# Head, tail and order of work of a four-stage sequence kernel: dummies and x, field 14's sums, and a table of shifts for the planner

## The chip, the cores and the metric

The kernel runs on one core of one Trainium2 chip. The metric is device microseconds (us) of one execution, the median of several. In the text PE is TensorE's matmuls and PEld its weight loads, DVE is VectorE, ACT is ScalarE, POOL is GpSimd and SP is the queue of SyncE, which here issues most DMA transfers.

## The reference

The input x holds 16 batches of 256 rows by 256 columns, float32. Four layers follow each other; each batch is independent, so a batch can be in one layer while the next is still in an earlier one.

```python
# layer 0: adapter with an expert per batch, residual, layer norm
hidden = gelu(x @ down_W.T + down_b)                       # 64 wide
hidden = hidden @ expert_W[idx].T + expert_b[idx] + domain_emb[idx]
x = ln(hidden @ up_W.T + up_b + x) * ln_gamma + ln_beta
# layer 1: transformer block, 16 heads of 16, scale and shift from a timestep
xn = ln(x) * (1 + scale) + shift
p = softmax(where(mask, -inf, q @ k.T / 4 + attention_bias))
x = xn + (p @ v) @ Wo + bo
x = x + gelu2((ln(x) * g2 + beta2) @ W1 + b1) @ W2 + b2    # 1024 wide
# layer 2: one of three branches per batch, residual, layer norm
y = ln(x + branch[c](x)) * gamma + beta
# layer 3: y as a 256 x 256 field, one explicit time step
df = -(grad(A0*y, 1) + grad(A1*y, 2)) + 0.5 * (grad2(B0*y, 1) + grad2(B1*y, 2) + 2 mixed terms of B2*y)
out = maximum(y + df * dt, 0)
```

The attention bias is the large operand: 16 x 16 x 256 x 256 float32.

## The kernel before

**Chains and a planner.** The work is written as ten Python generators, called chains: adapt and prepare (layer 0), project, weigh, attend, mask and divide (attention), enter and feed (its feed-forward half), end (layer 2) and step (layer 3). Each writes the instructions of its stage for batch after batch and stops at every `yield`, which names the time when its next piece can start and how many PSUM banks it needs. The class Flow (L99) keeps a clock for each engine and for the DMA engines, advanced by a fixed cost for each piece (`flow.dve(0.66)` and the like). `run` (L163) chooses which chain goes on: among those whose next piece can start by TensorE's planned clock, those in a hurry first, then the one with the lowest position `c[2]`; with none ready, the one that can start first. A position starts at a constant and grows with the TensorE time that the chain has spent (L1388 on, `flow.add(project(), -0.03998, 9.784)`: start, and TensorE us per unit of position). So the planner only fixes the order in which instructions are written. On the chip every engine runs its own instructions in that order, and waits by semaphores.

**PSUM and TensorE.** Seven banks are given out by `misc` and returned by `free`; an eighth holds the attention sums. A float32 product is two instructions of TensorE. Instructions named idle (L229 to L242) are products of zeros, which compute nothing that is used: they read `c_va`, two tiles that DVE clears at the start.

**The head.** The first batch goes through its stages nearly alone: w_down, xt and tokens are loaded; p_h (L565) is the first product, gelu follows on ACT, p_e (L580) needs the expert's weights, whose DMA (L323) needs the token's index, p_u (L596) leads back to 256 columns, and x is added on DVE (L604) after POOL has added up_b to it (`biased`, L550). `prepare` takes the means and variances (L438, L439), POOL makes rs from them (L442, L443), and then come `silus`, `condition` (ps_a, L521, which reads w_ada) and three dummies of 512 columns. `project` starts with the transposes c_t (L485) of c_ln. Loads of the head go out on SP's and ACT's queues in the order of the code: x of batch 0 on SP, behind xt; w_ada on ACT, ahead of rows_a.

**The body.** weigh writes the scores of four heads (c_s, L837 or L850), DVE adds the bias and takes the maximum (L870), ACT takes the exponential (L881); attend transposes (c_pt), copies to c_pts on DVE or ACT and multiplies with the values (c_c, L932). project makes q, k and v; from batch 1 on its halves go through DMA transfers (c_st, L658) before weigh can use them. feed has d_f (L1044), tanh, L1068 on DVE, and d_o (L1076) with the addition to y on DVE (L1085). end has d_g, gelu, d_y and the addition to y (L1218), and the means and variances for the last layer.

**The tail.** step works the fields. For fields 0 to 14 (loop at L1309) the normalization ends on POOL (L477, L478), and POOL makes all products and differences: w and a0 (L1318, L1319), a0's sums (L1322, L1323) and edges (L1274 to L1276), b0, p, q, w's sum and edges, and o (L1338). TensorE multiplies with the stencils (`along` L1286, `across` L1296), DVE adds w and the growth (`grown`, L1300, L1301), ACT clips, and SP's queue writes out. For field 14 the TensorE part is held back until end has done batch 15. Field 15 is written out by hand: its normalized field f lies in PSUM (`normalized_affine` with hurry: four instructions on DVE, L468 and L471), ACT copies it to y, DVE makes b0, a0, a0's sums through ps_w in PSUM, and POOL makes p, q and w at the same time; four dummies (`awake`, L1236) stand between field 14's products and its own.

Of the kernel before, what the change touches and what calls it, by code (L numbers as in the profile page):

```python
# [17 lines left out]
ALU = mybir.AluOpType  # L18
# [78 lines left out]


class Flow:  # L99

# [6 lines left out]
    def __init__(self, banks):  # L107
        self.clock = dict.fromkeys(self.LAG, 0.0) | {"SP": 15.5, "DMA": 22.0}
        self.chains = []
        self.after = self.spent = 0.0  # L110
        self.free_at = [0.0] * banks
        self.table = None
# [49 lines left out]

    def run(self):  # L163
        while self.chains:
            open_ = [c for c in self.chains if c[4] is None or c[4]()]
            assert open_, "no chain can go on"
            now = self.clock["PE"] + 0.02818
            ready = [c for c in open_ if self.start(c) <= now]
            if ready:
                c = min(ready, key=lambda c: (not c[5], c[2]))  # L170
            else:
                c = min(open_, key=lambda c: (self.start(c), not c[5], c[2]))
            self.after, self.spent = max(c[1][0], self.clock["PE"] if not ready else 0.0), 0.0
# [13 lines left out]
def chain_kernel(ctx: ExitStack, tc: tile.TileContext, t: dict, out: bass.AP):  # L187
# [39 lines left out]
    vas = [fixed(f"c_va{i}", [P, NC, H // 2, 4, HD]) for i in range(2)]  # L227
    for va in vas:
        nc.vector.memset(va, 0.0)  # L229
# [11 lines left out]
    idles = []  # L241
    idle(512, 384)  # L242

# [20 lines left out]
    def load_x(b):  # L264
        arrives["x", b] = flow.dma(0.8, freed.get(("x", b - 3), 0.0)) if b > 1 else 0.0
        xs[b] = xp.tile([P, NC, D], F32, name=f"x{b}", tag="x", bufs=3)
        nc.sync.dma_start(out=xs[b], in_=t["x"][b])

# [7 lines left out]
    w_ada = wp.tile([P, NC, 2 * D], F32, name="w_ada", tag="d_w", bufs=1)  # L276
    nc.scalar.dma_start(out=w_ada, in_=chunked(t["W_ada"]))
    smalls = hp.tile([P, NC * S], F32, name="smalls", tag="d_ln", bufs=1)
# [106 lines left out]

    rows_a = load("rows_a", rows(t["rows_a"]), [P, 5 * D])
    ln0_g, ln0_b, bv, bo, up_b = (rows_a[:, i * D : (i + 1) * D] for i in range(5))
    w_qkv = fixed("w_qkv", [P, NC, 3 * D])
# [220 lines left out]
    def prepare():  # L609
        for b in range(B):  # L610
# [10 lines left out]
            if b == 0:  # L621
                silus()
                condition()
                idle(512, 512, 512)
            yield at, 0
# [467 lines left out]
    ones = fixed("ones", [1, P])  # L1093
    nc.vector.memset(ones, 1.0)
    chosen = {}
# [130 lines left out]
    def step():  # L1226
# [81 lines left out]
        both = slice(0, NC)  # L1308
        for b in range(B - 1):  # L1309
            yield lambda: ("branch", b) in done  # L1310
# [29 lines left out]
            yield at_b  # L1340
            last = b == B - 2
            if last:
                yield lambda: ("branch", B - 1) in done
            ps_d = misc(f"e_d{b}", [P, NC, S])
            along(ps_d, h_m, b0, start=True)
            for w_, src in ((h_m, b0), (g_m, a0)):
                across(ps_d, w_, src)
            along(ps_d, g_m, a0, stop=True)
            at = flow.pe(2.93)
            if not last:  # L1350
                yield max(at, at_r), 0, True
                free(f"e_d{b}", grown(b, ps_d, w, o, both, 1.42, max(at, at_r)))
                done.add(("step", b))

        n = B - 1
        y, stat, at_y = stats3.pop(n)
        f, ps_w, ps_l = (misc(name, [P, NC, S]) for name in ("e_f", "e_ps_w", f"e_d{n}"))
        tmp, b0_, a0_, p_, q_, w_ = (wide(f"e_{x}{n}") for x in ("tmp", "b0", "a0", "p", "q", "w"))
# [4 lines left out]
        nc.scalar.copy(y, f)  # L1363
        flow.act(0.6, at_f)
        nc.vector.tensor_tensor(b0_, f, b0_g, ALU.mult)
        along(ps_l, h_m, b0_, start=True)
        across(ps_l, h_m, b0_)
        flow.pe(1.5, flow.dve(0.66, at_f))
        nc.gpsimd.tensor_tensor(p_, y, p_g, ALU.mult)
        nc.gpsimd.tensor_tensor(q_, y, q_g, ALU.mult)  # L1370
        nc.gpsimd.tensor_tensor(w_[:, :, mid], p_[:, :, right], q_[:, :, left], ALU.add)
        edges(nc.gpsimd, "r", n, y, edge_r, w_)
        at_w = flow.pool(4.5, flow.clock["ACT"])
        nc.vector.tensor_tensor(ps_w, f, w_g, ALU.mult)
        nc.vector.tensor_tensor(a0_, f, a0_g, ALU.mult)
        nc.vector.tensor_tensor(a0_[:, :, mid], a0_[:, :, mid], ps_w[:, :, right], ALU.add)
        nc.vector.tensor_tensor(a0_[:, :, mid], a0_[:, :, mid], ps_w[:, :, left], ALU.subtract)
        edges(nc.vector, "z", n, f, edge_z, a0_)
        across(ps_l, g_m, a0_)
        along(ps_l, g_m, a0_, stop=True)  # L1380
        at_l = flow.pe(1.4, flow.dve(3.2))
        grown(b, ps_d, w, o, both, 1.42, max(at, at_r))
# [14 lines left out]
    flow.add(step(), 4.348, 57.82)  # L1397
    flow.run()

# [87 lines left out]
```

## Time and profile before

| what | us |
|---|---|
| median of 3 runs (lowest, highest) | 825.84 (824.91, 828.47) |
| the profiled execution | 826.82 |
| its span, first to last instruction | 825.0 |
| TensorE busy in the span | 777.7 |
| mean granted TensorE clock | 0.981 |
| granted clock at one half, in the span | 12.6 to 26.2, 77.4 to 80.8, from 811.3 on |
| DMA traffic | 186.80 MB, mean 226 GB/s |

The page gives each engine's busy time, the span in 40 slices of 20.6 us with a digit for tenths of busy time, and the chain of work that ended last, followed back from the last instruction. Other views are the timeline, the busy time of each engine by stretches, and the waits with the instruction that ended them. A releaser is inferred, and a wait for several things is put down to the last of them.

### The profile page before, as it was taken

How to read it: one execution, taken by the hardware profiler on the slowest of the kernel's cores; microseconds unless marked ns; L12 is line 12 of the kernel's file. 1: busy time of each engine (PE TensorE's matmuls, PEld its weight loads, DVE VectorE, ACT ScalarE, POOL GpSimd, SP SyncE). 2: the span in 40 equal slices, each digit the busy share in tenths (PEclk: the TensorE clock that was granted, in tenths of full speed). 3: DMA queues.
4: the chain of work that ended last, by engine and by line, in shares of the span. 5: the costliest groups of instructions: out<-in, count | busy, mean ns of one | idle time of the engine just before them, and what ended most of it. 6: DMA issues, size and time to landing. Idle time of an engine off the chain costs nothing. (4 is left out here: it accounts for less than half of the span.)

```text
span 825.0 us, 17511 instructions
## 1 busy us (share of the span) xinstructions
PE 777.7 (94%) x5680; PEld 590.4 (72%) x5680; DVE 564.2 (68%) x1964; ACT 598.4 (73%) x1668; POOL 528.3 (64%) x726
## 2 busy tenths in 40 slices
PE   6987999999899999999999999999999999999995
PEld 3565777676677777777777778777777877778772
DVE  6576878787578695678777667766758666747335
ACT  2486889777678586979787579868778787768330
POOL 2437857865777657686266645929292496786885
PEclk8899999999999999999999999999999999999996
DMA  8979799699789988999976998589999989751110
GB/s 291 353 221 277 220 295 294 199 256 252 215 221 275 245 235 256 251 274 273 271 217 199 252 268 261 162 255 254 247 243 290 257 226 257 188 151 46 38 46 26
DMA packets 79242, 186.80 MB, mean 226 GB/s; under 512 B 8473, under 2 KB 22699, under 8 KB 71083
## 3 DMA queue, kind: packets, MB, share of 16 engines
q1 hardware_dynamic: 46192, 120.52, 42.7%
q0 software_dynamic: 31680, 62.92, 35.4%
q10 hardware_dynamic: 1275, 2.19, 0.7%
q8 instruction: 48, 0.79, 0.4%
q14 instruction: 47, 0.39, 0.1%
HBM read 94.90 MB, written 4.19 MB: 120 GB/s over the span
## 5 line engine op out<-in xcount | busy, mean ns | idle before, releaser
L881 ACT ACTIVATE c_pr<-c_pr,c_mx 128x256 f32<-128x256 f32 x512 | 254.8, 500 | 59.9 <-DVE c_mx L870 56.2
L870 DVE CUSTOM_DVE_ANT_0 c_pr<-c_s,side 128x256 f32<-128x256 f32 x512 | 190.8, 417 | 26.9 <-PE c_s L850 6.9
L485 PE MATMUL c_pt<-ident,c_pr 128*128 128x128 f32 x1024 | 155.5, 278 | 5.5 <-ACT d_ht L1021 1.0
L485 PEld LDWEIGHTS c_pt<-ident,c_pr 128*128 128x128 f32 x1024 | 116.5, 140 | 45.7 <-issue 17.1
L1044 PE MATMUL d_f<-d_ht,w 128*128 128x256 f32 x512 | 123.0, 383 | 2.4 <-ACT c_pts L495 0.8
L1076 PE MATMUL d_o<-w,d_z 128*128 128x256 f32 x512 | 120.6, 381 | 0.0
L493 DVE COPY c_pts<-c_pt 128x512 f32<-128x512 f32 x122 | 83.0, 685 | 52.8 <-PE c_pt L485 51.6
L442 POOL TENSOR_SCALAR rs<-mv 128x2 f32<-128x2 f32 x64 | 14.2, 221 | 162.7 <-DVE mv L439 157.1
L538 POOL DMA_DIRECT2D side<-neg x60 | 80.6, 1376 | 41.9 <-DMA side<-in_side 14.1
L1044 PEld LDWEIGHTS d_f<-d_ht,w 128*128 128x128 f32 x512 | 92.4, 190 | 17.5 <-DVE c_mx L870 2.5
L1076 PEld LDWEIGHTS d_o<-w,d_z 128*128 128x128 f32 x512 | 93.2, 190 | 11.7 <-issue 0.4
L881 ACT ACTIVATION_READ_ACCUMULATOR c_pr<-c_pr,c_mx 128x1 f32 x512 | 96.9, 189 | 0.0
L495 ACT COPY c_pts<-c_pt 128x512 f32<-128x512 f32 x134 | 76.7, 575 | 21.0 <-PE c_pt L485 20.6
L932 PE MATMUL c_c<-c_pts,c_va 128*32 128x256 f32 x1024 | 71.7, 385 | 6.3 <-ACT c_pts L495 3.4
L932 PEld LDWEIGHTS c_c<-c_pts,c_va 128*32 128x32 f32 x1024 | 27.6, 109 | 36.3 <-issue 13.3
L1068 DVE SCALAR_TENSOR_TENSOR d_z<-d_f,d_z 128x512 f32<-128x512 f32 x64 | 43.6, 680 | 12.3 <-ACT d_f L1064 12.0
L443 POOL TENSOR_TENSOR rs<-rs,inv_sqrt 128x2 f32<-128x2 f32 x64 | 46.1, 721 | 5.3
L850 PE MATMUL c_s<-c_st 32*128 32x256 f32 x960 | 46.9, 303 | 1.4 <-DVE x L604 0.5
L850 PEld LDWEIGHTS c_s<-c_st 32*128 32x128 f32 x960 | 33.5, 183 | 20.3 <-issue 11.5
L1064 ACT ACTIVATE d_f<-d_z 128x512 f32<-128x512 f32 x64 | 38.3, 598 | 10.3 <-DVE d_z L1061 8.5
L1061 DVE TENSOR_SCALAR d_z<-d_f,cols 128x256 f32<-128x256 f32 x82 | 35.8, 478 | 12.6 <-PE d_f L1044 12.5
L870 DVE DVE_READ_ACCUMULATOR2_ANT c_mx<- 128x1 f32 x512 | 42.5, 83 | 0.0
(195 smaller groups left out, 1490.9 us busy)
## 6 DMA issues: line engine op xcount, KB each, us to landing
side<-in_side SPq DMA_DIRECT2D x63, 1024.0 KB, 6.1
side<-neg POOLq DMA_DIRECT2D x60, 1024.0 KB, 10.2
c_st<-c_qk SPq DMA_DIRECT2D x60, 192.0 KB, 6.1
d_w<-in_W_branch SPq DMA_DIRECT2D x16, 512.0 KB, 6.0
c_st<-c_qk SPq DMA_DIRECT2D x60, 128.0 KB, 6.1
xt<-in_x_t SPq DMA_DIRECT2D x16, 256.0 KB, 5.2
x<-in_x SPq DMA_DIRECT2D x16, 256.0 KB, 5.4
c_st<-c_qk SPq DMA_DIRECT2D x60, 64.0 KB, 5.8
```

What stands on the lines that cost most here:

```text
L443: nc.gpsimd.tensor_tensor(rs, rs, inv_sqrt, ALU.pow)
L485: nc.tensor.transpose(ps[:, k, c * P : (c + 1) * P], src[:, c, k * P : (k + 1) * P], ident)
L493: nc.vector.tensor_copy(dst, ps)
L495: nc.scalar.copy(dst, ps)
L538: nc.gpsimd.dma_start(out=sides[m].rearrange("p (h c) k -> p h (c k)", h=HB), in_=negs[m // 4].rearrange("p c k -> p (c k)").unsqueeze(1). ...
L850: nc.tensor.matmul(ps[i][:, c, :], stacked[rows32, par, 0, c * P : (c + 1) * P], stacked[rows32, par, part, :], start=part == 1 and m not ...
L870: nc.vector.tensor_tensor_reduce(out=pr[:, c, :], in0=ps[i][:, c, :], in1=sb[:, i * NC + c, :], scale=-1.0, scalar=3.0e38, op0=ALU.add, op ...
L881: nc.scalar.activation(pr[:, c, :], pr[:, c, :], AF.Exp, bias=mx[:, c : c + 1], scale=-1.0, accum_out=sums[:, c, h : h + 1],)
L932: nc.tensor.matmul(ps_c[32 * i : 32 * i + 32, :], va[:, k, 4 * half + i, 2 * par : 2 * par + 2, :].rearrange("p e d -> p (e d)"), turned[i ...
L1044: nc.tensor.matmul(ps_f[:, i, :], w1[:, k, f * P : (f + 1) * P], h_t[:, k, :], start=k == 0, stop=k == NC - 1,)
L1068: nc.vector.scalar_tensor_tensor(z, ps_f, 1.0, z, ALU.add, ALU.mult)
L1076: nc.tensor.matmul(ps_o, us[f // 2][:, f % 2, c * P : (c + 1) * P], w2[:, f, :], start=f == 0, stop=f == NF - 1,)
```

## The change

It has four parts.

1. Head. The clearing of the two `c_va` tiles is swapped, so that the one that the dummies read comes first. The dummies ahead of p_h become three of 512 columns (512 and 384 before), those after `condition` four (three before). x of batch 0 is loaded by GpSimd's queue, w_ada goes out behind rows_a, and the tile of ones is set on GpSimd.
2. Field 14 is taken out of the loop and worked as field 15 is: f and ps_w in PSUM, its sums on DVE, p, q and w on GpSimd, o on DVE. Helpers `on_pool`, `on_dve` and `whole` hold what both fields, or the loop, share. What was in the loop for fields 0 to 13 stays.
3. `run` gets a table of 76 entries (plan time, chain, amount). When TensorE's planned clock reaches an entry's time, the amount is added to the position of that chain. Half of the amounts are smaller than 0.81 in size; the largest are those shown. Summed by chain: project +16.7, prepare +5.5, weigh +3.4, attend +0.2, feed -0.3, adapt -1.1, step -2.0, end -3.0, enter -5.3.
4. The planner's clocks start at 4.2 (0 before), SP's at 17.0 (15.5), that of the DMA engines at 23.0 (22.0).

```diff
+SHIFTS = [
+    (4.9, "weigh", -1.29),
+    (5.8, "prepare", 1.69),
+    (19.1, "end", -1.22),
+    (36.8, "weigh", 0.91),
+    (47.8, "end", -0.82),
+    (50.3, "project", 7.46),
+    (50.8, "enter", -0.03),
+    (63.7, "attend", 5.57),
+    (92.3, "step", 0.09),
+    (93.2, "attend", -2.73),
...
+    (160.3, "project", 6.37),
...
+    (841, "step", -2.69),
+]
...
-        self.clock = dict.fromkeys(self.LAG, 0.0) | {"SP": 15.5, "DMA": 22.0}
+        self.clock = dict.fromkeys(self.LAG, 4.2) | {"SP": 17.0, "DMA": 23.0}
...
-    def run(self):
+    def run(self, shifts=()):
+
+        shifts = list(shifts)
         while self.chains:
+            while shifts and shifts[0][0] <= self.clock["PE"]:
+                _, name, by = shifts.pop(0)
+                for c in self.chains:
+                    if c[0].__name__ == name:
+                        c[2] += by
...
-    for va in vas:
+    for va in vas[::-1]:
         nc.vector.memset(va, 0.0)
...
-    idle(512, 384)
+    idle(512, 512, 512)
...
-        nc.sync.dma_start(out=xs[b], in_=t["x"][b])
+        (nc.sync if b else nc.gpsimd).dma_start(out=xs[b], in_=t["x"][b])
...
-    nc.scalar.dma_start(out=w_ada, in_=chunked(t["W_ada"]))
...
     rows_a = load("rows_a", rows(t["rows_a"]), [P, 5 * D])
+    nc.scalar.dma_start(out=w_ada, in_=chunked(t["W_ada"]))
...
-                idle(512, 512, 512)
+                idle(512, 512, 512, 512)
...
-    nc.vector.memset(ones, 1.0)
+    nc.gpsimd.memset(ones, 1.0)
...
-        for b in range(B - 1):
+
+        def on_pool(b, y, p, q, w, at):
+
+            nc.gpsimd.tensor_tensor(p, y, p_g, ALU.mult)
+            nc.gpsimd.tensor_tensor(q, y, q_g, ALU.mult)
+            nc.gpsimd.tensor_tensor(w[:, :, mid], p[:, :, right], q[:, :, left], ALU.add)
+            edges(nc.gpsimd, "r", b, y, edge_r, w)
+            return flow.pool(4.5, at)
+
+        def on_dve(b, f, ps_w, a0):
+
+            nc.vector.tensor_tensor(ps_w, f, w_g, ALU.mult)
+            nc.vector.tensor_tensor(a0, f, a0_g, ALU.mult)
+            nc.vector.tensor_tensor(a0[:, :, mid], a0[:, :, mid], ps_w[:, :, right], ALU.add)
+            nc.vector.tensor_tensor(a0[:, :, mid], a0[:, :, mid], ps_w[:, :, left], ALU.subtract)
+            edges(nc.vector, "z", b, f, edge_z, a0)
+            return flow.dve(3.2)
+
+        def whole(ps, a0, b0):
+            along(ps, h_m, b0, start=True)
+            for w_, src in ((h_m, b0), (g_m, a0)):
+                across(ps, w_, src)
+            along(ps, g_m, a0, stop=True)
+            return flow.pe(2.93)
+
+        for b in range(B - 2):
...
+        b = B - 2
+        yield lambda: ("branch", b) in done
+        y, stat, at = stats3.pop(b)
+        yield at, 2
...
+        f, ps_w = (misc(f"{x}{b}", [P, NC, S]) for x in ("e_f", "e_pw"))
+        at_f = normalized_affine(f, y, stat, ln3_g, ln3_b, tmp, True)
+        nc.scalar.copy(y, f)
+        at_y = flow.act(0.6, at_f)
+        nc.vector.tensor_tensor(b0, f, b0_g, ALU.mult)
+        flow.dve(0.66)
+        at_w = on_pool(b, y, p, q, w, at_y)
+        yield 0.0, 0
+        at = on_dve(b, f, ps_w, a0)
+        free(f"e_pw{b}", at)
+        yield at_g, 0
+        nc.vector.tensor_tensor(o, f, grow, ALU.mult)
+        at_r = max(at_w, free(f"e_f{b}", flow.dve(0.66, at_g)))
+        yield at
+        yield lambda: ("branch", B - 1) in done
+        ps_d = misc(f"e_d{b}", [P, NC, S])
+        at = whole(ps_d, a0, b0)
...
-    flow.run()
+    flow.run(SHIFTS)
```

Field 15's part calls `on_pool` and `on_dve` in the places where the same instructions stood.

More of the change, by code (lines that the diff above doesn't have):

```diff
@@ L96 @@
     COLUMNS += _n
+SHIFTS = [
[9 more added lines that the diff above has]
+    (93.2, "attend", -2.73),
+    (99.9, "project", 0.79),
+    (108.6, "step", 1.18),
+    (139.2, "project", 0.71),
+    (145, "feed", 0.13),
+    (160.3, "project", 6.37),
+    (170.2, "prepare", 0.32),
+    (181.7, "step", -0.79),
+    (184.9, "step", -0.2),
+    (190.5, "prepare", 0.3),
+    (211.8, "adapt", -1.17),
+    (221.2, "step", 0.25),
+    (235.4, "weigh", 0.31),
+    (239.5, "enter", -1.33),
+    (255, "project", 0.64),
+    (262.2, "enter", -3.97),
+    (270.1, "project", -0.57),
+    (271.9, "attend", 0),
+    (280.5, "prepare", 2.44),
+    (292.6, "attend", -0.64),
+    (312.1, "weigh", 1.8),
+    (323.8, "feed", 0.56),
+    (359.7, "weigh", 0.9),
+    (377.5, "step", 0.53),
+    (394, "attend", -2.9),
+    (395, "end", 0.06),
+    (411.8, "project", 2.8),
+    (422.5, "prepare", 0.13),
+    (436.3, "feed", 0.13),
+    (457.1, "feed", -0.52),
+    (462.5, "step", -1.9),
+    (469.6, "attend", 0.19),
+    (486.6, "end", -0.02),
+    (496.6, "feed", -0.85),
+    (508.4, "prepare", -0.21),
+    (508.8, "weigh", 1.58),
+    (522, "feed", -0.57),
+    (538, "weigh", 0.55),
+    (543.7, "prepare", 0.26),
+    (551.8, "enter", -0.93),
+    (555.6, "step", -1.79),
+    (569.3, "project", -0.34),
+    (570.2, "prepare", -1.07),
+    (584, "step", 3.33),
+    (591.9, "prepare", -0.28),
+    (609.8, "prepare", 1.91),
+    (618, "enter", 0.04),
+    (628.8, "step", -0.44),
+    (633.1, "project", -1.14),
+    (633.7, "adapt", -1.65),
+    (649, "project", -1.04),
+    (657.8, "end", 0.32),
+    (668.1, "step", -0.14),
+    (685.6, "project", 1.23),
+    (691.9, "weigh", -0.94),
+    (702.8, "adapt", 1.75),
+    (711.7, "enter", 0.25),
+    (714.1, "end", -1.28),
+    (722.1, "attend", -0.42),
+    (728.6, "project", -0.21),
+    (742.9, "step", 2.79),
+    (748.5, "attend", 1.09),
+    (762.7, "enter", 0.67),
+    (774.1, "feed", 0.83),
+    (802.6, "step", -2.26),
+    (812.3, "weigh", -0.37),
+    (841, "step", -2.69),
+]
 class Flow:
@@ L1340, in step @@
             yield at_b
-            last = b == B - 2
-            if last:
-                yield lambda: ("branch", B - 1) in done
             ps_d = misc(f"e_d{b}", [P, NC, S])
[L1345 to L1353, printed above, removed]
+            at = whole(ps_d, a0, b0)
+            yield max(at, at_r), 0, True
+            free(f"e_d{b}", grown(b, ps_d, w, o, both, 1.42, max(at, at_r)))
+            done.add(("step", b))
+        b = B - 2
+        yield lambda: ("branch", b) in done
+        y, stat, at = stats3.pop(b)
+        yield at, 2
+        tmp, a0, b0, p, q = (wide(f"e_{x}{b}") for x in ("tmp", "a0", "b0", "p", "q"))
+        grow, at_g = growth(wide(f"e_grow{b}"), b)
+        w, o = (wide(f"e_{x}{b}") for x in ("w", "o"))
+        f, ps_w = (misc(f"{x}{b}", [P, NC, S]) for x in ("e_f", "e_pw"))
[14 more added lines that the diff above has]
+        ps_d = misc(f"e_d{b}", [P, NC, S])
+        at = whole(ps_d, a0, b0)
         n = B - 1
         y, stat, at_y = stats3.pop(n)
-        f, ps_w, ps_l = (misc(name, [P, NC, S]) for name in ("e_f", "e_ps_w", f"e_d{n}"))
+        f, ps_w, ps_l = (misc(f"{x}{n}", [P, NC, S]) for x in ("e_f", "e_pw", "e_d"))
         tmp, b0_, a0_, p_, q_, w_ = (wide(f"e_{x}{n}") for x in ("tmp", "b0", "a0", "p", "q", "w"))
@@ L1363, in step @@
         nc.scalar.copy(y, f)
-        flow.act(0.6, at_f)
+        at_y = flow.act(0.6, at_f)
         nc.vector.tensor_tensor(b0_, f, b0_g, ALU.mult)
@@ L1368, in step @@
         flow.pe(1.5, flow.dve(0.66, at_f))
[L1369 to L1378, printed above, removed]
+        at_w = on_pool(n, y, p_, q_, w_, at_y)
+        at_l = on_dve(n, f, ps_w, a0_)
         across(ps_l, g_m, a0_)
         along(ps_l, g_m, a0_, stop=True)
-        at_l = flow.pe(1.4, flow.dve(3.2))
+        at_l = flow.pe(1.4, at_l)
         grown(b, ps_d, w, o, both, 1.42, max(at, at_r))
```

## The prediction

> **What bounds the kernel now.** I read the page, then the busy time by stretches, then TensorE's waits, then the chain that ended last beside the timelines of the first 28 and last 25 us. The page's row of busy times, its TensorE slices and its clock row come first:
>
> ```profile
> PE 777.7 (94%) x5680; PEld 590.4 (72%) x5680; DVE 564.2 (68%) x1964; ACT 598.4 (73%) x1668; POOL 528.3 (64%) x726
> ...
> PE   6987999999899999999999999999999999999995
> ...
> PEclk8899999999999999999999999999999999999996
> ```
>
> TensorE is the bound: busy 777.7 of 825.0 us, idle 47.3; no other engine is above 73%. The stretches (columns: PE, PEld, DVE, ACT, POOL, granted clock, DMA share, GB/s) say where the idle time lies:
>
> ```profile
> 0.00:26.00 26.00, 18.14 (x56) 10.01 (x57) 16.25 (x58) 4.88 (x7) 9.35 (x20) 0.74 0.87 305
> 26.00:40.00 14.00, 13.05 (x97) 9.62 (x95) 7.17 (x28) 8.60 (x27) 3.65 (x8) 0.99 1.00 344
> 40.00:85.00 45.00, 37.13 (x293) 25.15 (x294) 30.60 (x118) 35.20 (x99) 25.41 (x40) 0.96 0.84 252
> 85.00:790.00 705.00, 685.44 (x5139) 529.39 (x5138) 495.16 (x1731) 542.40 (x1523) 468.28 (x630) 1.00 0.82 229
> 790.00:804.60 14.60, 13.22 (x60) 10.59 (x59) 3.18 (x8) 5.29 (x10) 11.45 (x15) 1.00 0.13 46
> 804.60:825.00 20.40, 10.74 (x40) 5.66 (x38) 11.86 (x24) 2.05 (x4) 10.17 (x17) 0.66 0.08 26
> ```
>
> By subtraction: 7.9 us idle in the head, 1.0 and 7.9 up to 85 us, 19.6 in the body, 1.4 and 9.7 in the tail. Dummies and x act on the head, the shifts on the body, field 14 on the tail.
>
> **Tail: fields 14 and 15.** The timelines of DVE, then POOL, then PE (start, duration, engine, line, operation; in brackets the idle time before and its releaser):
>
> ```profile
> 806.32 0.18 DVE L439 BATCH_NORM_AGGREGATE mv<-st 128x2 f32<-128x6 f32 x1
> ...
> 810.57 0.52 DVE L471 SCALAR_TENSOR_TENSOR e_f<-e_tmp,rs,rows_b 128x256 f32<-128x256 f32 x1 [2.99 <-POOL rs L443]
> ```
>
> ```profile
> 808.17 1.26 POOL L1338 TENSOR_TENSOR e_o<-y,e_grow 128x512 f32<-128x512 f32 x1
> 809.52 0.22 POOL L442 TENSOR_SCALAR rs<-mv 128x2 f32<-128x2 f32 x1
> ```
>
> ```profile
> 807.31 1.89 PE L1236 MATMUL awake<-grids,ident 128*128 128x256 f32 x8
> 813.41 2.08 PE L1286 MATMUL e_d<-e_b,grids 128*128 128x256 f32 x4 [4.21 <-DVE e_b L1365]
> ...
> 817.64 2.07 PE L1286 MATMUL e_d<-e_a,grids 128*128 128x256 f32 x4
> ```
>
> Field 15's means and variances are ready at 806.50, but POOL's two rs instructions queue behind field 14, which POOL works alone from 794.04 to 809.43, so that field 15's e_f waits. For field 14 itself the same two steps took from 791.13 (mv) to 792.24, 1.1 us. With POOL free, e_f starts at about 806.50 + 1.14 = 807.64 instead of 810.57: **2.93 us earlier**.
>
> Is POOL free? After the change POOL keeps p and q (1.27 each), w (1.08), the edges (about 0.8) and their gaps, 4.5 us, after ACT's copy (0.59). The affine step goes to DVE and can begin at 792.84, after the feed's L1068. By field 15's rows it takes 0.47 + 0.52 + 0.47 + 0.49 = 1.95 us, to 794.8; the copy ends at 795.4, POOL at about 800, 6 us ahead of need. Cover is ample.
>
> What DVE gains, by field 15's rows: 1.95, b0 0.69, sums and edges 812.66 + 0.61 to 816.60 (3.33), o 0.68: 6.65 us, to about 799.5. It was idle 6.63 us ahead of 804.61, but in that time stands the feed's last addition to y (L1085, 797.55), which TensorE's transpose, d_g, d_y and all of field 15 wait for. The planner writes field 14's pieces as soon as their inputs are due, and DVE runs in program order: if all stand ahead of both L1085 (0.42 each), the last begins at 799.9, not 797.55. So this order costs 0 to 2.4 us on the path. I take the middle, **+1.2**, since the trace shows neither order, and keep both ends.
>
> Behind e_f, TensorE's clock counts. The dummies "awake" end at 809.2, b0 comes 4.2 us later, and the granted clock fell at 811.3: four L1286 took 2.08 us where 1.10 is usual (782.29). Moved 2.93 us up, the first gap becomes 1.3 us and the next (b0's products done, a0 not) about 1.5; in any 3.41 us there are then some 1.7 busy. Windows of 3.41 us with 1.33 (807.87 on) and 1.55 busy (73.99 on) were followed by half clock, one with 1.53 (70.58 on) was not. So I expect full clock, barely. The last eight products then take 0.6 + 1.1 instead of 1.06 + 2.07, but DVE is itself busy until 815.5 (818.58 - 2.93 - a little), so **1.2 us** is won, not 1.4; bounds 0 and 1.4. The grown steps and the out transfers behind are as before.
>
> Tail sum: -2.93 + 1.2 - 1.2 = **-2.9**, bounds -4.3 and -0.5.
>
> Here two pages bear. The Trainium skill, "SBUF — State Buffer", section "SBUF: two separate sides", says that a DVE instruction with two SBUF inputs and a GpSimd instruction exclude each other for a whole instruction; that speaks against sums on both at once. The row that bears on it is L468 at 806.44: 1.14 us beside POOL's w, 0.47 at 811.01 without. Field 14's f and ps_w lie in PSUM, and the same sums of field 15 took 0.68 to 0.70 beside POOL's 1.27, so row and rule charge at most the small edges. By the rule without PSUM, four sums would add some 4 us. "TensorE: Matmul & The Clock Gate", section "Part 1: The HAM clock gate", says that an idle window of about 3.4 us brings half clock; by it a gap of 1.3 us is harmless and the 1.2 us are won. The third window above, 1.55 us busy and yet followed by half clock, says that the rule is too kind.
>
> **Head.** Reversing the memsets lets the dummies begin at 2.03 rather than 3.06 (one memset is 0.91). At the half clock that the dummies show, a 512-column product took two instructions of 0.85: three take 5.1, to 7.2, against 6.41 now. p_h (2.36) then ends near 9.6, gelu near 10.1; but p_e waits until 11.16 for the expert's weights (1.83 us idle, released by DMA), whose issue hangs on the tokens. So the dummies cost nothing; without that cover 0.8. x off SP's queue frees 0.33 us there, behind which only tokens matter: nothing. On POOL an issue costs about what the mask's does (1.38), ahead of ident, which nobody needs before 26. With x and rows_a earlier (rows_a no longer behind w_ada's issue, 4.39), POOL's L550 leaves 10.92 to 12.22, where DVE's L392 took 1.24 instead of 0.2 and h2 came 0.6 us after p_e's end: about **-0.5** to p_u and all behind it. w_ada, issued perhaps 1.5 us later and 5.6 in flight, still lands by 11 to 12, needed at 17.5. The memset of ones is 0.17.
>
> ```profile
> 20.93 5.44 PE L238 MATMUL idle<-c_va 128*128 128x512 f32 x6
> 26.18 0.62 PE L485 MATMUL c_t<-ident,c_ln 128*128 128x128 f32 x4
> ```
>
> c_ln is ready at 22.85, yet c_t stands behind three dummies at half clock; the clock rose at 26.2. A fourth adds 0.85 us at full clock, up to 1.7 at half: I take **+0.85**. Head sum **+0.3**, bounds -1.5 and +1.7.
>
> **Shifts.** They change no instruction's cost, only which ready chain is written next; with them go the planner's starting clocks. Every moved piece takes its DMA issues along: project moves the twelve c_st transfers on SP, weigh the next side loads, mask POOL's accumulating ones. The sum they can win is the idle time: 1.0 + 7.9 + 19.6 = 28.5 us, and a cold spell at 77.4 to 80.8 (d_t 1.39 and c_q 2.82, against 0.6 and 1.95: 1.6 us). The largest wait there:
>
> ```profile
> 75.14 0.33 PE L485 MATMUL c_t<-ident,c_ln 128*128 128x128 f32 x1 [3.03 <-ACT c_ln L459]
> ```
>
> c_t of batch 2 hangs on p_u (60.05), which stood behind c_q (52.16) and c_k (57.69) of batch 1. The largest entry, +7.46 for project at 50.3, lets adapt and attend go first just there; +5.57 for attend at 63.7 hands the place back. I take half of 7.9 + 1.6, 4.7 us. In the body the waits are scattered (the longest 1.9 us; TensorE's c_c and c_o on ACT and DVE), and half of the 76 entries move a chain by under 0.81: I take an eighth of 19.6, 2.4. Together **-7.1**. This is the uncertain term: at best the whole 9.5 and a third of 19.6 (-16), at worst a stall like that of 72 to 75 with its cold spell more (5.5) and half the body's idle again (10): +15.
>
> **The sum.** -2.9 + 0.3 - 7.1 = -9.7. The profiled execution took 826.82 us (span 825.0, 1.8 around it): 817.1. The median shown, 825.84, lies 0.98 lower: **816.0**.
>
> **Rivals.** (A) Waits only move: the shifts put one wait in another's place, since ACT and DVE chains of softmax still pace each quad. For it: 19.6 us over 705 is only 2.8%. Against: 7.9 in one place. Then the tail alone counts: 825.84 - 2.9 + 0.3 = 823.2; chance 0.15. (B) Slower: project, held back, delivers batch 1 late. c_s of batch 1 (76.11) came 16.4 us after c_k's end (59.7), through DVE's low halves and the c_st transfers; TensorE has nothing else from 72.1 to 75.1, and later feeds need batch 0 alone. Each us by which c_k ends later than 59.7 is paid once batch 0's work is out; from some 3 us on it eats the tail's gain. At 10 us: 825.84 + 10 - 2.9 = 833. Chance 0.13. (C) The tail doesn't do what it says: DVE's order costs 2.4 and the clock still falls: 825.84 - 0.5 + 0.3 - 7.1 = 818.5; still faster, 0.2. The forecast itself has 0.52.
>
> Low end: -16 from the shifts, -4.3 tail and -0.5 head make 805; I stop at 807. The high end takes in most of (B): 829. A difference of 0.5% (4.1 us) is about what a measurement of this kernel can tell from no change. Faster by more (under 821.7): forecast and (C), 0.72. Within: (A), 0.15. Slower: (B), 0.13.
>
> **What would show it.** Right: no wait of e_f on POOL's rs over 1 us; L1085's last start within 1.2 us of TensorE's last d_o; the last four L1286 near 1.1 us; p_u about 0.5 us earlier, first c_t near 26.5; idle in 40 to 85 near 4 us. Wrong: idle there unchanged or larger, half clock to the end, or batch 1's c_s later than 76 without other work before it.

## The result, and the profile after

The changed kernel took 837.77 us (median of 4 runs, 835.53 to 839.47) against 825.58 us for the kernel before (4 runs): **1.4% slower**, ratio 1.0139, 95% interval 1.0103 to 1.0175. The forecast was 816.0 us, faster. The profiled execution took 838.82 us with a span of 837.0, 12.0 more than before.

From the page of the changed kernel, the row of busy times and the slices of TensorE and of its clock:

```profile
PE 788.2 (94%) x5684; PEld 595.0 (71%) x5684; DVE 574.7 (69%) x1988; ACT 593.4 (71%) x1655; POOL 519.0 (62%) x717
...
PE   6978899989998999999999999999999999999986
...
PEclk7889999999999999999999999999999999999986
```

TensorE's share is still 94%. Of the 12.0 us only 1.5 are new idle time (47.3 to 48.8); 10.5 are new *busy* time. The only new instructions of TensorE are four of dummies, two rows of 512 columns, some 1 us in the head. So something made products take longer. The stretches (columns as in the prediction: PE, PEld, DVE, ACT, POOL, granted clock, DMA share, GB/s):

```profile
0.00:27.40 27.40, 19.19 (x60) 10.31 (x61) 16.74 (x57) 4.87 (x7) 10.56 (x24) 0.75 0.84 293
27.40:40.00 12.60, 11.05 (x73) 8.32 (x71) 5.84 (x23) 7.01 (x23) 4.03 (x7) 1.00 1.02 356
40.00:85.00 45.00, 38.16 (x294) 24.75 (x292) 34.03 (x124) 30.12 (x82) 23.53 (x37) 0.92 0.66 201
85.00:797.00 712.00, 690.74 (x5161) 532.05 (x5162) 497.52 (x1740) 543.84 (x1533) 469.69 (x632) 1.00 0.83 230
797.00:808.50 11.50, 8.63 (x40) 7.11 (x39) 9.45 (x22) 3.34 (x7) 5.53 (x10) 0.97 0.22 57
808.50:837.00 28.50, 20.45 (x63) 12.43 (x61) 11.14 (x24) 4.20 (x8) 5.70 (x10) 0.62 0.05 18
```

The wait that the shifts were to remove (40 to 85 us) went from 7.9 to 6.8 us idle, not to 4, and the clock there fell from 0.96 to 0.92. In the last row TensorE is busy 20.45 us at a clock of 0.62: that is the tail at half speed. The execution can be cut into three stages at two events, the first c_t and the end of the last d_o:

| stage (us, one profiled execution each) | before | after | difference |
|---|---|---|---|
| to the first c_t | 26.2 | 27.5 | +1.4 |
| first c_t to the end of d_o | 771.3 | 777.3 | +6.0 |
| end of d_o to the end of the span | 27.5 | 32.2 | +4.7 |

**Tail.** The timeline of DVE in the changed kernel, then that of TensorE:

```profile
800.07 0.48 DVE L555 SCALAR_TENSOR_TENSOR e_tmp<-y,mv,rows_b 128x256 f32<-128x256 f32 x1
...
802.78 0.69 DVE L1470 TENSOR_TENSOR e_b<-e_f,grids 128x512 f32<-128x512 f32 x1 [0.71 <-ACT y L1468]
803.39 0.69 DVE L1407 TENSOR_TENSOR e_pw<-e_f,grids 128x512 f32<-128x512 f32 x1
...
806.63 0.68 DVE L1477 TENSOR_TENSOR e_o<-e_f,e_grow 128x512 f32<-128x512 f32 x1
807.23 0.74 DVE L1172 SCALAR_TENSOR_TENSOR y<-d_o,y 128x256 f32<-128x256 f32 x2
```

```profile
802.73 2.11 PE L1163 MATMUL d_o<-w,d_z 128*128 128x256 f32 x9
807.70 1.23 PE L572 MATMUL d_t<-ident,y 128*128 128x128 f32 x4 [2.87 <-DVE y L1172]
809.61 3.78 PE L1255 MATMUL d_g<-d_xt,d_w 128*128 128x256 f32 x8 [0.67 <-ACT d_xt L582]
813.54 2.04 PE L1292 MATMUL d_y<-d_bout,ones 1*128 1x256 f32 x4
815.51 3.78 PE L1296 MATMUL d_y<-d_w,d_hid 128*128 128x256 f32 x8
...
828.57 1.06 PE L1383 MATMUL e_d<-e_a,grids 32*32 32x256 f32 x4 [1.55 <-DVE e_a L1363]
829.57 2.08 PE L1373 MATMUL e_d<-e_a,grids 128*128 128x256 f32 x4
```

All of field 14's work on DVE stands ahead of the feed's last addition to y (L1172, L1085 before), which so ends 3.1 us after d_o instead of 0.5. TensorE is idle for 2.87 us; from 807.85 to 821.5 the granted clock is one half, and d_g and d_y take 3.78 us each where they took 1.99. At 828.33 the clock falls again, ahead of the last eight products. What was hoped for came too: POOL waits for field 15 instead of being late,

```profile
821.31 0.36 POOL L529 TENSOR_SCALAR rs<-mv 128x2 f32<-128x2 f32 x1 [14.07 <-DVE mv L526]
```

so from the ready means to e_f it is 1.28 us instead of 4.07. Step by step from the end of d_o: first d_t +2.9 us, from there to the end of d_y +4.5, means to e_f -2.8, the rest +0.1: +4.7.

**Head.** DVE and POOL of the changed kernel, then TensorE:

```profile
10.11 1.20 DVE L445 TENSOR_SCALAR smalls<-smalls 128x16 f32<-128x16 f32 x1
11.35 0.17 DVE L446 TENSOR_SCALAR smalls<-smalls 128x16 f32<-128x16 f32 x1
```

```profile
10.02 1.26 POOL L637 TENSOR_TENSOR x<-x,rows_a 128x512 f32<-128x512 f32 x1 [6.82 <-DMA rows_a<-in_rows_a]
```

```profile
8.25 1.08 PE L652 MATMUL p_h<-xt,w_down 128*64 128x256 f32 x6 [1.00 <-DMA xt<-in_x_t]
14.02 2.08 PE L683 MATMUL p_u<-up,a_h 64*128 64x256 f32 x8 [0.95 <-DVE a_h L669]
...
21.92 5.80 PE L325 MATMUL idle<-c_va 128*128 128x512 f32 x8
27.55 0.60 PE L572 MATMUL c_t<-ident,c_ln 128*128 128x128 f32 x4
```

POOL's addition to x did leave its old place, but came to lie beside another small DVE instruction of the same chain: L445 took 1.20 us, its neighbour of the same shape 0.17. p_u began 0.97 us later than before; 0.4 of it was there ahead of this, as the first DVE instruction that needs `cols` began at 6.70 instead of 6.26. The fourth row of dummies ahead of c_t (two instructions) did the rest, 0.4 us.

**Body.** The weight loads of c_pt, what their sequencer waited for (us in total, times), after and then before:

```profile
L572 PEld LDWEIGHTS c_pt<-ident,c_pr x1024: 137/140/183, 36.1 to 771.1; 128*128 128x128 f32 x171
...
  ACT c_pr L968: 12.9, 26
```

```profile
L485 PEld LDWEIGHTS c_pt<-ident,c_pr x1024: 137/140/145, 34.7 to 761.8; 128*128 128x128 f32 x171
...
  ACT c_pr L881: 2.0, 6
```

Transposes now come up before their exponentials are done, 26 times instead of 6. Taking each product's time as the part in which no earlier one was still under way, the 1024 c_pt took 133.0 us instead of 129.5. This is no chance of one execution: in the ten profiles below whose body is written in the old order or nearly so, the sum is 129.2 to 129.6 us and the wait for exponentials 2.0 to 2.1. With 6.8 instead of 3.4 us of half clock (50.1 to 56.9), this is most of the busy time that the body gained (idle there rose only from 28.4 to 29.6).

### The profile page after: what moved, and what is told of

Read it like the earlier page. It is cut to its first block, busy times and chain, and to the rows that moved or that the text cites. A ratio compares the mean times of both kernels' runs of the same rounds, so it can differ in the third digit from the quotient of the medians.

```text
span 837.0 us, 17554 instructions
## 1 busy us (share of the span) xinstructions
PE 788.2 (94%) x5684; PEld 595.0 (71%) x5684; DVE 574.7 (69%) x1988; ACT 593.4 (71%) x1655; POOL 519.0 (62%) x717
## 5 line engine op out<-in xcount | busy, mean ns | idle before, releaser
L957 DVE CUSTOM_DVE_ANT_0 c_pr<-c_s,side 128x256 f32<-128x256 f32 x512 | 190.8, 416 | 32.1 <-DMA side<-neg 12.2
L572 PE MATMUL c_pt<-ident,c_pr 128*128 128x128 f32 x1024 | 159.4, 279 | 10.6 <-ACT c_pr L968 5.3
L580 DVE COPY c_pts<-c_pt 128x512 f32<-128x512 f32 x117 | 79.9, 686 | 41.9 <-PE c_pt L572 40.1
L1131 PEld LDWEIGHTS d_f<-d_ht,w 128*128 128x128 f32 x512 | 92.4, 190 | 15.5 <-ACT c_pts L582 1.3
L582 ACT COPY c_pts<-c_pt 128x512 f32<-128x512 f32 x139 | 79.2, 576 | 14.8 <-PE c_pt L572 14.2
L1148 DVE TENSOR_SCALAR d_z<-d_f,cols 128x256 f32<-128x256 f32 x96 | 41.9, 478 | 19.9 <-PE d_f L1131 19.6
L1155 DVE SCALAR_TENSOR_TENSOR d_z<-d_f,d_z 128x512 f32<-128x512 f32 x64 | 43.4, 679 | 11.3 <-ACT d_f L1151 10.5
```

What stands on the lines that cost most here:

```text
L572: nc.tensor.transpose(ps[:, k, c * P : (c + 1) * P], src[:, c, k * P : (k + 1) * P], ident)
L580: nc.vector.tensor_copy(dst, ps)
L582: nc.scalar.copy(dst, ps)
L957: nc.vector.tensor_tensor_reduce(out=pr[:, c, :], in0=ps[i][:, c, :], in1=sb[:, i * NC + c, :], scale=-1.0, scalar=3.0e38, op0=ALU.add, op ...
L1131: nc.tensor.matmul(ps_f[:, i, :], w1[:, k, f * P : (f + 1) * P], h_t[:, k, :], start=k == 0, stop=k == NC - 1,)
L1155: nc.vector.scalar_tensor_tensor(z, ps_f, 1.0, z, ALU.add, ALU.mult)
```

## The experiments

Ratios are against runs of the kernel before made on the same chip beside them (medians 826.7 to 828.3 us), with 95% intervals. Stages are in us, from one profile each.

| kernel | ratio | to c_t | to end of d_o | tail |
|---|---|---|---|---|
| e1_tail | 1.0033 (1.0012 to 1.0054) | 25.0 | 772.7 | 32.1 |
| e2_head | 1.0026 (1.0002 to 1.0050) | 26.4 | 777.8 | 27.5 |
| e3_plan | 1.0097 (1.0065 to 1.0130) | 25.5 | 779.7 | 27.5 |
| e4_tail_held | 0.9974 (0.9950 to 0.9999) | 25.4 | 773.9 | 23.9 |
| e5_clocks | 1.0697 (1.0649 to 1.0745) | 25.4 | 823.2 | 32.3 |
| e6_all_held | 1.0062 (1.0039 to 1.0086) | 26.8 | 777.1 | 24.2 |
| e7_project | 1.0442 (1.0403 to 1.0481) | 25.5 | 809.7 | 24.6 |
| e8_others | 1.0260 (1.0224 to 1.0297) | 25.3 | 796.4 | 25.0 |
| e9_late | 1.0265 (1.0222 to 1.0308) | 25.6 | 799.1 | 24.7 |
| e10_dma1 | 1.0478 (1.0450 to 1.0506) | 26.6 | 808.3 | 27.8 |
| e11_one | 0.9985 (0.9962 to 1.0007) | 25.5 | 771.2 | 27.4 |
| e12_best | 0.9965 (0.9947 to 0.9983) | 25.5 | 772.8 | 23.2 |
| e13_dummies | 1.0028 (1.0002 to 1.0053) | 25.9 | 775.1 | 27.5 |
| e14_x | 1.0007 (0.9987 to 1.0027) | 25.5 | 772.6 | 27.5 |
| e15_best | 0.9944 (0.9917 to 0.9972) | 26.3 | 771.7 | 23.2 |
| e16_one_late | 1.0049 (1.0030 to 1.0068) | 26.6 | 776.2 | 27.4 |
| e17_row1 | 0.9968 (0.9945 to 0.9990) | 21.8 | 773.5 | 23.2 |
| e18_row2 | 0.9954 (0.9932 to 0.9975) | 24.3 | 773.8 | 23.2 |

### The three parts, each alone

e1_tail is the kernel before with field 14 worked as in the change; e2_head has the head's edits alone; e3_plan has the table and the planner's new clocks alone.

> The kernel before with field 14's part of the change alone; every engine's instructions are the same and in the same order up to field 14. Theory 1 (the tail loses by the order on DVE: the feed's last additions to y stand behind field 14's sums and o, TensorE then waits some 2.5 us and drops to half clock under d_g and d_y): about +4.7 us on 825.6, so 830, with TensorE's transpose d_t waiting over 2 us for y. Rival A (the shifts alone make the change slower, field 14's part wins what was forecast): -2.9, so 822.7. Rival B (DVE and GpSimd block each other while both make sums): field 14's DVE sums take over 1 us each instead of 0.7.

> The kernel before with the head's part alone (dummies, clearing order, x on GpSimd's queue, w_ada behind rows_a, ones on GpSimd); the order of all other instructions is unchanged. Theory 1: the first c_t comes about 1.4 us later, as in the changed kernel (27.55 against 26.18), and that reaches the end: +1.4, 827.0. Rival A: +0.3 or less, 825.9. If the body takes up the delay in waits that are there anyway: 825.6.

> The kernel before with the table of shifts and the planner's starting clocks alone, field 14 in the loop as before. Theory 1 (three terms that add: head 1.4, tail 4.7, the rest of 12.2 by the order): +6, 831.7. Rival A: +12 to +15, 838 or more, since head and tail would win. If the order is neutral: 825.6.

Each part loses by itself: 0.33, 0.26 and 0.97%, together 1.56 where the whole lost 1.39. The head's interval only just clears 1. The largest is the part that the forecast credited with most of the gain. e1 shows the changed kernel's tail to 0.1 us (32.1), so the tail's loss has nothing to do with the plan ahead of it. In e2's profile the loss lies in the body, whose written order is the old one; that the head's edits caused it is not shown.

### The tail mended

```diff
-        yield 0.0, 0
+        yield lambda: ("feed", B - 1) in done
         at = on_dve(b, f, ps_w, a0)
```

e4_tail_held is e1 with this condition, which moves the two L1085 ahead of field 14's sums on DVE and changes nothing else; e6_all_held is the whole change with it.

> As the first run, but field 14's sums on DVE are written only after the feed's last two additions to y of batch 15; nothing else moves on any engine. Theory 1: the wait of d_t for y falls to 0.4 us as before, field 15's rs no longer waits on POOL, so the win of 2.9 us shows: 822.7, and 821.5 if the clock stays full behind it. Rival B (the shared access of DVE and GpSimd costs the time): no faster than the first run, about 830.

> The whole change with one more condition: field 14's sums on VectorE are not issued before the last field's operand y stands, as in the tail-held run. Theory T (the tail's loss is VectorE's order and the half clock that TensorE's idle 2.9 us brings, and has nothing to do with the plan ahead of it): the stage from the end of d_o to the end of the span falls from the 32.2 us of the changed kernel to 23.9 us, and the time by 8.3 us, from 837.8 to 829.5 us, which is still 3 to 4 us over the kernel before since the head's +1.4 and the body's +6 us stay. Rival (the tail-held run was short because its body ended luckily, with other operands ready): the tail stays over 27 us and the time over 833 us.

In e6, TensorE between the end of d_o and d_y:

```profile
804.46 0.55 PE L572 MATMUL d_t<-ident,y 128*128 128x128 f32 x3 [0.41 <-DVE y L1172]
805.68 1.99 PE L1255 MATMUL d_g<-d_xt,d_w 128*128 128x256 f32 x8 [0.68 <-ACT d_xt L582]
```

The wait of 2.87 us is 0.41, d_g is back at 1.99, and the tail is 24.2 us (23.9 in e4), 8 us shorter than in the changed kernel. Its ratio falls from 1.0139 to 1.0062; e3's +0.97% and e4's -0.26% add up to +0.71. By the medians of ten runs each on one chip, e4 is 5.8 us faster than e1. So one place in DVE's order decides whether the field's move is worth -3.6 us or +4.7. e4 is faster than the kernel before by 0.26%, an interval that just clears 1. Its last products still ran partly at half clock, from 816.3 on. e12_best adds one row to the four of `awake` ahead of field 15's first products, and three between its two groups:

```diff
-        awake(256, 256, 256, 256)
+        awake(256, 256, 256, 256, 256)
...
         flow.pe(1.5, flow.dve(0.66, at_f))
+        awake(256, 256, 256)
         at_w = on_pool(n, y, p_, q_, w_, at_y)
```

> The tail-held version of the tail part alone, with five instead of four rows of 256-column dummies ahead of the last field's first products and three such rows between its two product groups. In the tail-held run the clock was low from 816.3 to 825.2 us of the span, over the last products. Theory (idle TensorE in the last 10 us lets the clock fall, dummies there keep it): the last products run at full clock, the stage from d_o to the end is 1 to 2 us shorter than 23.9 us, the time about 824.5 us. Rival (the dummies stand in front of products that are ready, or the clock falls from waits elsewhere): 0 to 1 us longer than the tail-held run, 826 to 827 us.

The last products of e4, then of e12:

```profile
815.48 0.62 PE L1296 MATMUL e_d<-e_a,grids 32*32 32x256 f32 x4 [1.55 <-DVE e_a L1276]
816.03 1.83 PE L1286 MATMUL e_d<-e_a,grids 128*128 128x256 f32 x4
```

```profile
812.93 1.56 PE L1236 MATMUL awake<-grids,ident 128*128 128x256 f32 x6
814.56 0.62 PE L1296 MATMUL e_d<-e_a,grids 32*32 32x256 f32 x4
815.11 1.13 PE L1286 MATMUL e_d<-e_a,grids 128*128 128x256 f32 x4
```

The last four products took 1.13 instead of 1.83 us. The tail is 23.2 us, 0.6 shorter and not the 1 to 2 expected, as in e4 only the last group had been slow.

### The plan taken apart

All of these leave the work as it is and change only the order in which it is written.

```diff
 # e5_clocks: new starting clocks, no table
+        self.clock = dict.fromkeys(self.LAG, 4.2) | {"SP": 17.0, "DMA": 23.0}
 # e7_project: 12 entries of project, e8_others: the other 64,
 # e9_late: the 49 entries from 280 us on, all with the old clocks
+    flow.run(SHIFTS)
```

> The kernel before with the planner's starting clocks alone (4.2, 17.0, 23.0), no table. The order of the changed plan departs from the order before at TensorE's 77th product, at about 36 us, and that is due to these clocks, since a table that starts at 50.3 cannot move it. Theory C (the clocks make the early loss: batch 0's softmax ends near 69 us instead of 62.6, TensorE's transposes c_pt wait for exponentials): +4 to +6, so 832 to 834. Theory P (holding project back makes the loss): +0 to +1. Theory L (a tuned order loses by any disturbance, whatever it is): +5 to +8.

> The kernel before with only the 12 entries for project (+16.7 in all, the largest 7.46 and 6.37), old clocks. Theory P: +5 to +7, with c_q and c_k of batches 1 to 4 later and DVE idle before their scores. Theory C: +0 to +2. Theory L: +5 to +8.

> The kernel before with the 64 entries for the other chains, old clocks. Theory P and theory C: within 2 us of 826 to 828. Theory L: +5 to +8.

> The kernel before with the 49 entries from 280 us on, old clocks; up to there the order is the one before. In the traces of the changed plan nearly all of TensorE's extra waits for exponentials (12 of 13 us) lie before 280 us. If the loss is made there (theories P and C): within 2 us of the kernel before. Theory L: +4 to +8.

Every subset costs far more than the whole: clocks 7.0%, project 4.4, the others 2.6, the late ones 2.65, but clocks and table together 1.0. No expectation came near: the highest was 8 us, measured were 21 to 56. The entries are no independent improvements; the table fits these clocks and little else. e5's expectation says that the table starts at 50.3 us; it starts at 4.9. The early departure does come from the clocks all the same: e3 and e5 leave the old order at the same product, at 36 us, and e8, with the old clocks, at 84.

The tails of e7 to e9 show the forecast's 2.93 us from another side. Field 14 is worked there as in the kernel before, but POOL began its o 3.2 to 3.9 us after the end of d_o instead of 10.7, rs no longer stood behind it, and the tail took 24.6 to 25.0 us instead of 27.5. Two controls followed, with the clock of the DMA engines raised by 1.0 us and nothing else, and with single entries of the table:

```diff
 # e10_dma1
-        {"SP": 15.5, "DMA": 22.0}
+        {"SP": 15.5, "DMA": 23.0}
 # e11_one:       SHIFTS = [(99.9, "project", 0.79)]
 # e16_one_late:  SHIFTS = [(555.6, "step", -1.79)]
```

> The kernel before with one number of its plan changed: the planned clock of the DMA queues starts at 23.0 instead of 22.0 us. No work is added or taken away and the estimates are no worse than before; the order of TensorE's instructions changes from number 161 on. Theory L (the written table of shifts fits one order only, and any other order costs tens of us, whatever moved it): 20 to 55 us slower, 846 to 881 us, with the loss in c_pt's waits and in idle TensorE between 85 and 500 us of the span. Rival S (what costs is the direction or size of the change's own shifts, up to 4.2 us; a shift of 1 us is within the plan's own error): within 6 us of the kernel before, 820 to 832 us.

> The kernel before with one entry of the table alone, 0.79 us on the projecting chain at 99.9 us of the plan, and its old clocks. TensorE's order changes only from instruction 1321 to 1355 (four products of a projection go 26 places ahead) and is the old one again behind them; VectorE's and ScalarE's change by some five instructions. Theory L (an order that departs from the tuned one costs by the length over which it departs): within 3 us of the kernel before. Rival (any touch of the order makes the run fall out of step with its transfers and stay there): over 10 us slower.

> The kernel before with one entry of the table alone, -1.79 us on the growing chain at 555.6 us of the plan, and its old clocks. TensorE's order departs at instruction 3057 of 4298, at about 570 us, and stays changed up to 4180, over some 230 us. Theory L: the runs that depart for longer lost 0.03 to 0.07 us for each us of departed order (clocks alone 56 us over 780, the DMA clock 40 over 770, the late entries 22 over 510), so 7 to 16 us slower, 834 to 843 us. Rival S (it is the size of the shift that costs; one of 1.8 us on one chain is within the plan's error): within 3 us of the kernel before.

e10: +4.8% for 1 us in one number, so the size of a shift is not what costs. e11: none, so neither is it any touch. e16: +0.5%, 4.1 us, little more than half of the lowest expected for a cost by length; that part of the theory doesn't hold as a rule (0.02 us for each us of departed order here, 0.05 in e10). Where e10 lost it can be read from its trace. The stretches 250 to 500 us and from there to the end of d_o (PE busy, granted clock, DMA share, GB/s), e10 and then before:

```profile
250.00:500.00 250.00, 235.64 (x1735) 0.97 0.85 234
500.00:834.80 334.80, 320.23 (x2305) 0.99 0.70 192
```

```profile
250.00:500.00 250.00, 242.69 (x1855) 1.00 0.90 251
500.00:797.50 297.50, 293.37 (x2133) 1.00 0.71 198
```

Idle 14.4 and 14.6 us instead of 7.3 and 4.1. The largest wait in it, on TensorE, DVE and POOL:

```profile
483.68 1.09 PE L485 MATMUL d_t<-ident,d_ln 128*128 128x128 f32 x4 [7.35 <-DVE x L604]
```

```profile
482.84 0.69 DVE L604 TENSOR_TENSOR x<-p_u,x 128x512 f32<-128x512 f32 x1 [11.14 <-POOL x L550]
```

```profile
481.40 0.20 POOL L1276 TENSOR_TENSOR e_w<-e_rh 128x4 f32<-128x4 f32 x1
481.55 1.26 POOL L550 TENSOR_TENSOR x<-x,rows_a 128x512 f32<-128x512 f32 x1
```

The addition of up_b to x (L550) is 1.26 us of work, but in POOL's order it now stands behind the products of a field (step), and DVE, which also runs in its order, stands at L604 for 11.1 us with everything that TensorE needs behind it. e5 shows the same pair at 388 us (11.91 on DVE, 11.89 on TensorE). The rest of the losses has no such single place, but two sums hold most of it. In the wait above the clock fell, and it stayed at one half from 481.2 to 494.9. In all, the body of e10 (c_t to the end of d_o) has 31.4 us at half clock, where the kernel before has 3.4; e5, e7, e8 and e9 have 41.2, 30.7, 24.1 and 23.9. Let half of TensorE's busy time in these spells count as lost (an estimate, from d_g's 3.78 us against 1.99). Together with the added idle time this makes up all but 3 to 6 us of what each of the five bodies lost:

| body, us more than before | e5 | e7 | e8 | e9 | e10 |
|---|---|---|---|---|---|
| all | 51.9 | 38.3 | 25.0 | 27.7 | 37.0 |
| idle time | 32.2 | 21.9 | 14.4 | 13.6 | 21.5 |
| half clock, estimate | 14.1 | 11.1 | 8.0 | 9.8 | 11.8 |

In e3 and e16 it is waiting inside busy time, as in the changed kernel: c_pt's weight loads waited for exponentials, e3 first:

```profile
L572 PEld LDWEIGHTS c_pt<-ident,c_pr x1024: 137/140/231, 34.0 to 771.4; 128*128 128x128 f32 x171
...
  ACT c_pr L968: 13.1, 27
```

```profile
L497 PEld LDWEIGHTS c_pt<-ident,c_pr x1024: 137/140/229, 35.2 to 765.4; 128*128 128x128 f32 x171
...
  ACT c_pr L893: 5.3, 15
```

e3 also has three half-clock spells of 3.4 us between 49 and 179 us, where the kernel before has one. In e16 the stretch behind 570 us has 228.6 us of busy TensorE instead of 225.0 for the same products, and 4.3 instead of 2.5 idle.

### The head taken apart

e13_dummies has the reversed clearing, three longer dummies ahead of p_h and four rows instead of three ahead of c_t. e14_x has the other half: x on GpSimd's queue, w_ada behind rows_a, the ones on GpSimd. e15_best is e12 with e13's edits; e17 and e18 are e15 with one and two rows ahead of c_t.

```diff
 # e15_best           e17_row1        e18_row2
-                idle(512, 512, 512)
+                idle(512, 512, 512, 512)
+                                     idle(512)       idle(512, 512)
```

> Of the head part only the dummies and the reversed order of the value products; x stays on SyncE's queue, the ones stay on VectorE and the W_ada load keeps its place. Theory X (the head's +1.4 us comes from x on GpSimd's queue, which delays tokens and e_w and pushes GpSimd's up_b sum beside VectorE's small angle operations): p_u as before within 0.2 us, c_t later by the fourth dummy's 0.0 to 0.9 us only, time +0 to +0.9 us if the rest keeps its lead. Rival D (the three longer dummies ahead of p_h hold p_h back): p_u 0.4 us or more later than before, c_t 1.2 us or more later. Either may be covered by the spread of several us that the body shows from its transfers, so the stage up to c_t decides, not the time.

> Of the head part what the run with the dummies left out: x on GpSimd's queue, the W_ada load behind the small ones, the ones on GpSimd; the old dummies and the old order of the value products. Theory X (the head's loss comes from here, the run with the dummies having c_t at 25.9 us): e_w or the angle chain later, p_u at 13.2 us or more, c_t at 26.4 to 27.4 us, time +0.5 to +2 us. Rival (the head part costs nothing by itself and the 27.55 us of the changed kernel is the spread between executions): c_t at 25.4 to 26.2 us and the time within 1 us of the kernel before.

> What the runs so far favour, together: the tail-held version with dummies between the last field's products, and the head's dummies with the reversed value products; no shifts, old clocks, x on SyncE's queue. If the two add up: the stage up to c_t at 25.3 to 25.9 us, the stage from d_o on at 23.2 us, time 823 to 824 us, 0.3 to 0.5 per cent below the kernel before. Rival (the head's dummies are lost again in the waits on transfers of the first 100 us): as the version without them within 1 us, no better than 824 us.

> The combined best version with one row of dummies instead of four ahead of the first c_t; the order of everything else is the same. In the profile of that version c_ln was written by 23.2 us and c_t began at 26.3 us, when the dummies ended, 3 us later. Theory F (the dummies ahead of c_t hold it back, and more of them, as in the change, hold it back further): c_t at 23.3 to 23.6 us; the clock is then still low for 2 to 4 us of products, which gives 1 to 2 us back, so 1 to 2 us faster, about 822 us. Rival K (the dummies buy the full clock, and without them the low clock lasts until the first batch's scores, with new waits behind it): no gain or up to 3 us lost, 824 to 827 us.

> The same with two rows instead of four. Theory F: c_t at 24.2 to 24.6 us and half the gain, about 823 us. Rival K: within 1 us of the version with four rows.

Theory X falls: x on GpSimd's queue alone had c_t at 25.5 us and no loss (1.0007). c_t does follow the rows, as Theory F says. e15, then e17:

```profile
21.24 5.23 PE L238 MATMUL idle<-c_va 128*128 128x512 f32 x8
26.30 0.60 PE L485 MATMUL c_t<-ident,c_ln 128*128 128x128 f32 x4
```

```profile
19.91 2.05 PE L238 MATMUL idle<-c_va 128*128 128x512 f32 x2
21.75 1.05 PE L485 MATMUL c_t<-ident,c_ln 128*128 128x128 f32 x4
```

But the time doesn't follow c_t: 0.9944, 0.9954 and 0.9968 with four, two and one rows, intervals that overlap. c_t's 2 to 4.5 us were given back, as Rival K had it; where was not found (e17's stages are those of its fastest run, 820.26 us, the median is 823.93). And e13 lost 0.28% by itself, while the same edits on top of e12 (e15) lost nothing, so a ratio of that size is at the edge of what these runs tell. So the head's +1.4 us of the table above can't be taken as time lost. Its spread says the same: with the old head, twelve profiles (that of before among them) have c_t between 25.0 and 26.6 us, the median 25.5; with the new one the three have 26.4, 26.8 and 27.5. For p_u the old head has 12.2 to 13.5, the new one 13.2, 13.2 and 14.0.

## Why the prediction was wrong

**The shifts were mis-signed (forecast -7.1, bounds -16 to +15; e3 alone +0.97%, some 8 us; body stage +6.0).** The step that failed is "The sum they can win is the idle time", with the sentence before it that shifts change no instruction's cost. In the changed kernel idle time hardly moved (28.4 to 29.6); the loss came as busy time, c_pt's 3.5 us behind weight loads that wait for exponentials, and products at half clock. (The body's +6.0 is from one profile, and such stages spread by over 6 us; e3's ratio and the c_pt sums carry the reading.) The idle time of 40 to 85 us did shrink (7.9 to 6.8), but adapt's p_u for batch 1, let forward, waited for its own input on DVE, and the clock was at one half from 50.09 on:

```profile
50.91 2.08 PE L683 MATMUL p_u<-up,a_h 64*128 64x256 f32 x8 [2.97 <-DVE a_h L669]
```

Scattered small waits were credited with a gain of an eighth, and no order tried here gained: of ten kernels with a body in another order, the changed one among them, nine lost 0.5 to 7.0% and one, which departs over 34 instructions, nothing.

**The tail's mechanism was named, its price was not (forecast -2.9, measured +4.7).** The 2.93 us from POOL's rs came (2.8). DVE's order, taken at +1.2 with an end at 2.4, cost 2.9: the end came, and a little more. Field 14's work began where it was assumed, right behind the feed's L1155 (L1068 before) and 4.8 us ahead of d_o's end (800.07; 792.84 was 4.7 ahead), but took 7.2 us instead of 6.65, with 0.71 of waiting for ACT's copy of y. The term that the sum lacked is what this idle time does to the clock: +4.5 us in d_t to d_y. Rival C let the clock fall, but only over the last eight products. The 1.2 us there didn't come either: e_d's last four took 2.08 us after a gap of 1.55. The forecast took some 1.7 us of busy TensorE in a window of 3.41 us to be enough, barely; the window up to 828.33 has 1.79, and half clock followed. What was right is the size of the win without these two: with DVE's order mended the tail gains 3.6 us (e4), and with rows of dummies in the gaps, which the change lacks, 4.3 (e12); -2.93 and -1.2 make -4.1. Choosing the middle between two orders was the mistake; the planner could have been followed by hand, since `yield 0.0, 0` makes the next piece ready at once.

**The head (forecast +0.3; c_t +1.4 in the profile).** "About -0.5" for p_u failed, as DVE's stretched instruction moved from L392 to L445 instead of vanishing: +0.97. In e2 and e6, with the same head, p_u is at 13.2, so most of the 0.97 is one execution's. The fourth row, taken at +0.85, put c_t 0.4 us further from the first dummy (5.63 instead of 5.25), as the clock rose at 26.2 in both, and was worth nothing in time.

**The rivals.** (A), waits only move, was nearest for idle time and wrong in price. (B) was the right sign, not the mechanism: batch 1's c_k ended 1.7 us later (61.4 instead of 59.7), less than the 3 us at which it decides, and though its first c_s came at 82.0 instead of 76.1, TensorE had other work up to then (2.2 us idle between 60 and 82). The locks between DVE and POOL, weighed in the prediction and charged at little, stayed away: field 14's sums took 0.68 to 0.69 us beside POOL's products,

```profile
802.83 1.27 POOL L1399 TENSOR_TENSOR e_p<-y,grids 128x512 f32<-128x512 f32 x1 [2.68 <-ACT y L1468]
804.05 1.28 POOL L1400 TENSOR_TENSOR e_q<-y,q_g 128x512 f32<-128x512 f32 x1
```

with f in PSUM. The Trainium skill's "SBUF — State Buffer", section "SBUF: two separate sides", has a GpSimd instruction shut out a DVE one for its whole length where that runs in a two-port mode or has two SBUF inputs. L445, 1.20 us beside POOL's 1.26, is in line with it, though the trace doesn't tell its mode.

**What stays open.** That a departing order costs here is shown for nine orders. Why is read from the profiles and not shown: for the two largest single waits (11 us each on DVE) from POOL's order, for c_pt from the waits of its weight loads, for the rest from sums of idle time and half clock. No experiment put POOL's L550 or the exponentials back alone, since any change of one chain's place rewrites the rest.

## What to carry to other kernels

When a planner writes the order, treat its order as one tuned object: a list of small improvements taken from it, or a 1 us change in one estimate, can be a new draw and no gain, as all of them were here, and waits that it brings can hide in TensorE's busy time. Before giving an engine work that was elsewhere, find in its program order what stands behind it and who waits for that; one condition in the right place turned this tail from 4.7 us lost into 3.6 us won. And price an idle gap ahead of dependent products by the clock that follows it, not by its own length: here 2.9 us idle cost 4.5 us more.

## What was not expected of the hardware

The clock fell after a window that wasn't idle: in the 3.41 us up to 807.85 TensorE was busy for 0.54 us, and its longest idle time was 2.87. The Trainium skill's "TensorE: Matmul & The Clock Gate", section "Part 1: The HAM clock gate", asks for an idle window of about that length. The measurement is stricter than that rule, and it decides: in e4 half clock followed at 816.3 behind a window with 1.86 us busy and no gap over 1.55. Nor is there a plain limit of busy time: the window with 1.53 us busy that the prediction names was not followed by it.

Ten kernels share the body's written order or nearly so (e1, e2, e4, e11 to e15, e17, e18); in their profiles the stage from c_t to d_o took 771.2 to 777.8 us. In the longest, e2, DVE stood 4.34 us ahead of the L870 at 406.67, for something that the profile doesn't name, and TensorE 2.49. A single profile therefore can't rank bodies closer than some 6 us, and only the runs' medians carry the verdicts above.
